# The first 12 alignments in four column blocks on 96 partitions, with rows joined through DRAM

## The chip, the cores and the metric

The kernel runs on one core of one Trainium2 chip. The metric is the device time of one execution in microseconds (us). Engines are named as in the profile: PE (TensorE), DVE (VectorE), ACT (ScalarE), POOL (GpSimd), SP (SyncE, which here only issues DMAs). Every engine works through its own instructions in a fixed order and waits at semaphores; 16 DMA engines move data.

## The reference, cut to what matters

The input x is 32 samples of 128 rows by 128 columns. Four steps update it: a gated attention, a quantized dense layer, an alignment (dynamic time warping) against ctx, and a mixture of 8 experts whose gates need one threshold over all 32 samples.

```python
x = x + tanh(g_xattn[0]) * _L0_xattn_ref(_layernorm(x), ctx_1024, ctx_1024, ...)
x = x + tanh(g_ffn[0])   * _L0_ffn_ref(_layernorm(x), W1, b1, W2, b2)
x = x + tanh(g_xattn[1]) * _L1_xattn_ref(ctx_1024, _layernorm(x))
x = x + tanh(g_ffn[1])   * _L1_ffn_ref(_layernorm(x), gate_weight, w1, b1, w2, b2)

def _align_one(small, large):                      # once for each of 32 samples
    D = sqrt(max(|small_i|^2 + |large_j|^2 - 2 small_i . large_j, 0))
    R[i, j] = D[i, j] + min(R[i-1, j], R[i, j-1], R[i-1, j-1])
    # walk back from the last corner to (0, 0): at each cell go to the smallest of
    # diagonal, up, left; every cell (i, j) on the way adds small[i] to expanded[j]
    return expanded
```

## The kernel before

**Before the alignment.** Attention and the first half of the quantized dense layer take the span up to about 220 us. The second half of the dense layer (`dense`, `second_dense`) is done in eight blocks of four samples, and each block's distances D follow from it. Samples 0 to 11 (blocks 0 to 2, `NP = 3`, `BP = 12`) are the first part, the other 20 the second part.

**Distances (L1134 to L1159).** For each of blocks 0 to 2, PE makes d2, DVE adds and clips (dd), ACT takes roots into `dist` (two buffers), and two DMAs write `dist` to `d_dram`, laid out as half, sample, row, column. Each sample is cut in two halves of `SH = 64` rows: the upper one from the top, the lower one upside down and reversed, so that both are scanned in the same direction. 12 samples by 2 halves are 24 lanes, one a partition.

**Rows (`warp_steps`, L955).** In chunks of 12 rows (the last has 4) SP loads the distances into `dc`. A row is two DVE instructions over 24 partitions by 128 columns: u = min(up, diagonal) at L1058, and a scan along the row, min with the left neighbour and add of the distance, at L1059. Results go into `ru`, as pairs (R, u) for each row.

**Tables (`tables`, L962).** The walk back needs for each cell the column in which the row above is reached. It is five DVE instructions over rows of R and u: dg (L975), to (L976), lf (L979), the scan vv (L982), dv (L986). To use more lanes, SP copies each finished chunk from `ru` to `rblk`, three rows to each of four partition groups (96 partitions, L1073), the tables are made while the next chunk is scanned, and SP moves dv back to 24 partitions into `DV` (memory of YT, L992).

**Meet and walk.** `meet` (L1000) turns the last rows by PE, joins the two halves and finds the cheapest crossing. `near`, the tables of the last four rows, is made on 24 partitions straight from `ru`. The walk is 63 dependent DVE instructions `hit` (L1087), one a row. Then PE turns the result (vt, ends_ps), and `ends` is ready (L1112). Ten matmuls `busy` (L953) run on PE shortly before the end of the walk; their result is not used.

**Beside it.** `second_dense` (from L1239) works through blocks 3 to 7 for the second part: ACT quantizes and takes norms and roots, PE makes po, tp and d, POOL adds, takes a power and stores the distances to `d_dram`. Its instructions are tied to one order on ACT (`last["act"]`) and PE (`last["pe"]`). Its place against the rows on PE and SP comes from the scheduler.

**After it.** The expert stage starts with `aligned(0)` (L1314) and the expert matmuls mph (L1494) and mpo (L1507). The second part's alignment (20 samples, 40 lanes) runs there in the background, with the same `warp_steps`; it begins with SP loading `dc` from `d_dram`.

What sets the order: within an engine, the scheduler puts instructions into one fixed order when the program is built, mostly in program order but by its own estimate of when an operand is ready; `tc.issue_after` adds an earliest place. DMAs take one of eight completion semaphores in turn, so that a ninth waits for the first.

Of the kernel before, what the change touches and what calls it, by code (L numbers as in the profile page):

```python
# [8 lines left out]
F32 = mybir.dt.float32  # L9
BF16 = mybir.dt.bfloat16  # L10
# [3 lines left out]
ALU = mybir.AluOpType  # L14
AX = mybir.AxisListType
# [3 lines left out]
P = 128  # L19
B = 32  # L20
S = 128
# [7 lines left out]
GB = 4  # L29
# [3 lines left out]
BIG = 1e30  # L33
SH = S // 2
# [3 lines left out]
NP = 3  # L38
BP = NP * GB
HELD = 34  # L40


@with_exitstack
def tile_flamingo_gated(
# [21 lines left out]
    nc = tc.nc  # L66
# [6 lines left out]
    def new(p, shape, dt, tag, bufs=None):  # L73
        kw = {} if bufs is None else {"bufs": bufs}
        return p.tile(shape, dt, tag=tag, name=tag, **kw)

    keep = pool(ctx, "keep")
    dram = pool(ctx, "dram", space=DRAM)
# [43 lines left out]
    ident = new(keep, [P, P], F32, "ident")  # L122
# [5 lines left out]
    rev = new(keep, [P, P], F32, "rev")  # L128
# [161 lines left out]
    with ExitStack() as st:  # L290
# [47 lines left out]
        for k in range(2):  # L338
# [5 lines left out]
                out=mtmp[:, k], in_=mtmp[:, k], compare_op=ALU.is_ge, fill=0.0,  # L344
# [444 lines left out]

    aa_s = new(rest, [P, B], F32, "aa_s")  # L790
    d_dram = new(dram, [2, B, SH, S], F32, "d_dram")
    parts = [ExitStack(), ExitStack()]
    HT = [None] * 4
    for k in (1, 0):
# [157 lines left out]
            with tc.issue_after(getattr(tie, "ins", tie)):  # L952
                tie = nc.tensor.matmul(busy, lhsT=onesb, rhs=w1q, start=True, stop=True)  # L953

    def warp_steps(s0, n_s, wp, w1p, ps_new, queue, DV, ends, lower, warmed=None):  # L955

        H2 = 2 * n_s
        BL = 2 if n_s > 16 else 4
        rows = max(n for _, n in CHUNKS)
        waiting = None  # L960

        def tables(rb, m, w, tag):  # L962


            lf, to = (new(w1p, [w, m, S + 1], BF16, t + tag) for t in ("lf", "to"))
            nc.vector.memset(lf[:, :, 0:1], 0.0)
            nc.vector.memset(to[:, :, 0:1], 0.0)
            dg = new(w1p, [w, m, S], BF16, "dg" + tag)
            vv = new(w1p, [w, m, S + 1], BF16, "vv" + tag)
            dv = new(w1p, [w, m, S], BF16, "dv" + tag)  # L970
            up = rb[:, 0:m, 0, 1 : S + 1]
            diag = rb[:, 0:m, 0, 0:S]
            left = rb[:, 1 : m + 1, 0, 0:S]
            least = rb[:, 1 : m + 1, 1, 0:S]
            nc.vector.tensor_tensor(dg, diag, up, ALU.is_le)  # L975
            nc.vector.tensor_tensor(  # L976
                to[:, :, 1:], jotab[0:w].unsqueeze(1).to_broadcast([w, m, S]), dg, ALU.subtract
            )
            nc.vector.tensor_tensor(lf[:, :, 1:], left, least, ALU.is_lt)  # L979


            nc.vector.tensor_tensor_scan(  # L982
                vv.rearrange("p r j -> p (r j)"), lf.rearrange("p r j -> p (r j)"),
                to.rearrange("p r j -> p (r j)"), 0.0, ALU.mult, ALU.min,
            )
            nc.vector.tensor_tensor(dv, vv[:, :, 1:], vv[:, :, 0:S], ALU.subtract)  # L986
            return dv

        def moved_tables(r0, m, rb):
            dv = tables(rb, m, BL * H2, "")  # L990
            for q in range(BL - 1, -1, -1):
                queue.dma_start(  # L992
                    out=DV[:, r0 + q * m : r0 + q * m + m, :], in_=dv[H2 * q : H2 * q + H2]
                )
# [1 line left out]
        vw = new(w1p, [H2, SH + 1], F32, "vw")  # L996
        nc.vector.memset(vw[:, 0:1], -2.0 * S)
        prev = None

        def meet(row):  # L1000

            gt_ps = ps_new([P, 2, n_s], "gt_ps")
            nc.tensor.transpose(gt_ps.rearrange("p h b -> p (h b)"), row, ident[0:H2, 0:H2])

            gt = new(w1p, [P, 2, 2, n_s], F32, "gt")
            nc.vector.tensor_copy(gt, gt_ps.unsqueeze(2).to_broadcast([P, 2, 2, n_s]))
            both_ps = ps_new([H2, 2, S], "both_ps")
            for h, where in ((0, ident), (1, rev)):
                nc.tensor.matmul(
                    both_ps[:, h, :], lhsT=gt[:, h].rearrange("p k b -> p (k b)"), rhs=where,  # L1010
                    start=True, stop=True,
                )
            far = new(w1p, [H2, S + 1], F32, "far")
            nc.vector.memset(far[:, S : S + 1], BIG)
            nc.vector.tensor_copy(far[:, 0:S], both_ps[:, 1, :])
            best = new(w1p, [H2, S], F32, "best")
            nc.vector.tensor_tensor(best, far[:, 0:S], far[:, 1 : S + 1], ALU.min)
            nc.vector.tensor_tensor(best, best, both_ps[:, 0, :], ALU.add)
            least = new(w1p, [H2, 1], F32, "least")
            nc.vector.tensor_reduce(least, best, AX.X, ALU.min)  # L1020
            to = new(w1p, [H2, S], F32, "far_to")
            nc.vector.tensor_tensor(to, far[:, 1 : S + 1], far[:, 0:S], ALU.is_le)
            nc.vector.scalar_tensor_tensor(to, to, 2.0, jota[0:H2], ALU.mult, ALU.add)
            cand = new(w1p, [H2, S], F32, "cand")
            nc.vector.scalar_tensor_tensor(cand, best, least, jota[0:H2], ALU.is_le, ALU.mult)
            mine = new(w1p, [H2, 1], F32, "mine")
            nc.vector.tensor_reduce(mine, cand, AX.X, ALU.min)
            got = new(w1p, [H2, 1], F32, "got")
            nc.vector.scalar_tensor_tensor(
                cand, jota[0:H2], mine, to, ALU.is_equal, ALU.mult, accum_out=got  # L1030
            )

            nc.vector.tensor_scalar(got, got, lower[:, 0:1], lower[:, 1:2], ALU.mult, ALU.add)
            nc.vector.scalar_tensor_tensor(
                vw[:, SH : SH + 1], mine, lower[:, 2:3], got, ALU.mult, ALU.add
            )

        for r0, n in CHUNKS:
            dc = new(wp, [H2, rows, S], F32, "dc")[:, 0:n, :]
            for v in (slice(0, 4), slice(4, n)) if r0 == 0 else (slice(0, n),):  # L1040
# [34 lines left out]
                    )  # L1075
                waiting = (r0, m, rb)
        yield 2.0
        meet(ru[:, n, 0, 1 : S + 1])
        yield 4.0
        near = tables(ru, n, H2, "_l")  # L1080
        yield 0.85 * n

        for r in range(SH - 1, 0, -1):
            hit = new(wp, [H2, S], BF16, "hit")
            nc.vector.scalar_tensor_tensor(  # L1087
                hit, jotab[0:H2], vw[:, r + 1 : r + 2],
                near[:, r - r0, :] if r >= r0 else DV[:, r, :], ALU.is_le, ALU.mult,
                accum_out=vw[:, r : r + 1],  # L1090
            )
            if warmed is not None and r == 12:
                idle(warmed, None, hit, 10)
            yield 0.39

        vt = ps_new([SH, 2, 2, n_s], "vt")
        for k in range(2):
            nc.tensor.transpose(
                vt[:, k].rearrange("p h b -> p (h b)"), vw[:, k : SH + k], ident[0:H2, 0:H2]
            )  # L1100
        ev = new(w1p, [SH, 2, 2, n_s], F32, "ev")
        nc.vector.tensor_copy(ev[:, 0], vt[:, :, 0])
        for k in range(2):
            nc.vector.tensor_scalar(
                ev[:, 1, k, :], vt[:, 1 - k, 1], -1.0, -2.0 * S - 2.0, ALU.mult, ALU.add
            )
        ends_ps = ps_new([P, 2, n_s], "ends_ps")
        for h, where in ((0, ident), (1, rev)):
            nc.tensor.matmul(
                ends_ps, lhsT=where[0:SH, :], rhs=ev[:, h], start=(h == 0), stop=(h == 1)  # L1110
            )
        nc.vector.tensor_copy(ends, ends_ps)  # L1112
        yield 1.0

    ends = [new(rest, [P, 2, n], F32, f"ends{n}_{k}") for k, n in enumerate((BP, B - BP))]

# [1 line left out]
    with ExitStack() as st:  # L1118
# [18 lines left out]
        for g, ym2, ysq in normed:  # L1137
            d2 = new(dps, [P, GB, S], F32, "d2")
            nc.tensor.matmul(d2, lhsT=ones, rhs=ysq, start=True, stop=False)  # L1139
            for i in range(GB):  # L1140
                nc.tensor.matmul(
                    d2[:, i, :], lhsT=CD[:, GB * g + i, :], rhs=ym2[:, i, :],
                    start=False, stop=(i == GB - 1),
                )
            dd = new(dp, [P, GB, S], F32, "dd")
            for i in range(GB):
                b = GB * g + i
                nc.vector.tensor_scalar(
                    dd[:, i, :], d2[:, i, :], aa[:, b : b + 1], 0.0, ALU.add, ALU.max
                )  # L1150
            dist = new(dp, [P, GB, S], F32, "dist")
            nc.scalar.activation(dist[0:SH], dd[0:SH], AF.Sqrt)
            got = nc.scalar.activation(dist[SH:P], dd[SH:P, :, ::-1], AF.Sqrt)
            held["root"] = getattr(got, "ins", got)
            for h in range(2):
                (nc.sync, nc.scalar if g == NP - 1 else nc.sync)[h].dma_start(
                    out=d_dram[h, GB * g : GB * g + GB].rearrange("b r j -> r b j"),
                    in_=dist[SH * h : SH * h + SH],
                )  # L1159
    parts[0].close()  # L1160


# [1 line left out]
    with ExitStack() as st:  # L1164
# [123 lines left out]
                d2 = distance_product(n, ym2, ysq)  # L1288
            roots(NG - 1, d2)

        for _ in warp_steps(
            0, BP, wp, w1p, lambda shape, tag: new(w_ps, shape, F32, tag), nc.sync,
            DV, ends[0], masks[0], new(w_ps, [P, HID], F32, "busy"),
        ):
            pass
# [270 lines left out]
```

## Time and profile before

| what | us |
|---|---|
| three runs | 858.38, 862.26, 864.83 |
| median | 862.26 |
| profiled execution: span | 854.5 |
| profiled execution: own time | not given; median less span is 7.8 |
| DVE busy / PE busy / ACT busy in the span | 591.8 / 690.8 / 449.7 |

The places of the stage in the profiled span:

| event | us |
|---|---|
| first store of distances issued on SP | 248.02 |
| first row scan | 258.77 |
| last row done, turned by PE (gt_ps) | 322.04 |
| first hit / first hit that reads moved tables | 328.47 / 334.13 |
| last hit done | 357.8 |
| ends written | 359.9 |
| first expert matmul (mph) | 370.24 |

How to read it: the profile gives busy time, idle time before an instruction and the releaser that ended it. A busy share over the whole span says little about this stage: from 248 to 358 us PE is mostly idle and DVE is nearly full; after 370 us PE is full and DVE has room.

### The profile page before, as it was taken

How to read it: one execution, taken by the hardware profiler on the slowest of the kernel's cores; microseconds unless marked ns; L12 is line 12 of the kernel's file. 1: busy time of each engine (PE TensorE's matmuls, PEld its weight loads, DVE VectorE, ACT ScalarE, POOL GpSimd, SP SyncE). 2: the span in 40 equal slices, each digit the busy share in tenths (PEclk: the TensorE clock that was granted, in tenths of full speed). 3: DMA queues.
4: the chain of work that ended last, by engine and by line, in shares of the span. 5: the costliest groups of instructions: out<-in, count | busy, mean ns of one | idle time of the engine just before them, and what ended most of it. 6: DMA issues, size and time to landing. Idle time of an engine off the chain costs nothing.

```text
span 854.5 us, 13313 instructions
## 1 busy us (share of the span) xinstructions
PE 690.8 (81%) x4721; PEld 459.1 (54%) x4721; DVE 591.8 (69%) x2052; ACT 449.7 (53%) x791; POOL 66.7 (8%) x132
## 2 busy tenths in 40 slices
PE   5798998344242435589999999999999999999997
PEld 2244454211231223257777777766777777777776
DVE  7757999879858998889993666656705544444444
ACT  3787877496258888334444443443443433434332
POOL 2000000000401221100101010010010000000000
PEclk9897999555565555699999999999999999999999
DMA  8100000200021221023543020020013112121110
GB/s 326 38 2 13 2 3 2 80 20 0 0 42 36 55 61 32 13 60 98 157 138 100 38 87 25 38 74 32 31 63 87 50 37 87 38 65 56 52 51 26
DMA packets 20201, 47.32 MB, mean 55 GB/s; under 512 B 4014, under 2 KB 6942, under 8 KB 20110
## 3 DMA queue, kind: packets, MB, share of 16 engines
q1 hardware_dynamic: 14372, 29.69, 11.4%
q0 software_dynamic: 5056, 16.62, 6.2%
q8 instruction: 37, 0.61, 0.3%
q10 hardware_dynamic: 706, 0.16, 0.1%
q14 instruction: 30, 0.25, 0.1%
HBM read 27.12 MB, written 13.37 MB: 47 GB/s over the span
## 4 chain that ended last, share of the span: by engine, by line
PE 55%; DVE 20%; issue 2%; DMA 1%; ACT 1%; POOL 0%; SPq 0%; DVEq 0%; ACTq 0%
PE mph L1494 25%; PE mpo L1507 25%; DVE ru L1059 4%; DVE ru L1058 3%; DVE hit L1087 2%; DVE hst L858 2%; DVE hst L859 2%; PE px L1328 1%; PE small L1357 1%; PE px L1351 1%; DVE junk L1371 1%; PE po L916 1%; DMA d_dram<-dist 1%; PE busy L953 0%; PE d L1139 0%
## 5 line engine op out<-in xcount | busy, mean ns | idle before, releaser
L1507 PEld LDWEIGHTS mpo<-mw,hT 128*128 128x128 f32 x2048 | 249.7, 192 | 58.9 <-issue 39.7
L1499 ACT ACTIVATE hT<-mph,mb1s 128x512 f32<-128x512 f32 x256 | 175.6, 687 | 181.9 <-PE mph L1494 168.4
L1507 PE MATMUL mpo<-mw,hT 128*128 128x128 f32 x2048 | 256.3, 276 | 0.1
L1494 PE MATMUL mph<-YT,mw 128*128 128x512 f32 x512 | 244.1, 597 | 0.0
L1494 PEld LDWEIGHTS mph<-YT,mw 128*128 128x128 f32 x512 | 87.2, 192 | 57.9 <-issue 57.8
L1457 DVE TENSOR_TENSOR biased<-mpo,mb2s 128x512 f32<-128x512 f32 x28 | 19.4, 691 | 119.6 <-PE mpo L1507 119.6
L1462 DVE SCALAR_TENSOR_TENSOR X<-biased,GA,X 128x128 f32<-128x128 f32 x248 | 67.8, 344 | 0.1
L1515 ACT COPY ye<-mpo 128x512 f32<-128x512 f32 x34 | 19.9, 585 | 86.1 <-PE mpo L1507 83.5
L1059 DVE TENSOR_TENSOR_SCAN ru<-ru,dc 24x128 f32<-24x128 f32 (+1 forms) x128 | 54.0, 422 | 6.9 <-DMA dc<-d_dram 3.2
L1058 DVE TENSOR_TENSOR ru<-ru 24x128 f32<-24x128 f32 (+1 forms) x128 | 38.9, 304 | 3.2
L1516 POOL DMA_DIRECT2D y_dram<-ye x34 | 18.5, 543 | 224.9 <-ACT ye L1515 224.5
L562 ACT ACTIVATE dm<-bi 128x512 f32<-128x512 f32 x48 | 28.8, 603 | 7.9 <-PE bi L557 2.7
L604 DVE TENSOR_TENSOR sm<-sc,dm 128x512 f32<-128x512 f32 x32 | 21.7, 682 | 12.8 <-ACT dm L562 9.7
L1209 PE MATMUL po<-w2q,HT 128*128 128x128 bf16 x80 | 9.4, 311 | 25.5 <-ACT HT L1182 25.5
L849 PE MATMUL ph<-XQ,w1q 128*128 128x512 bf16 x32 | 15.8, 616 | 16.6 <-DVE XQ L840 9.2
L1276 PE MATMUL tp<-ident,y 128*128 128x128 f32 x20 | 8.1, 474 | 22.6 <-ACT y L1182 22.6
L1087 DVE SCALAR_TENSOR_TENSOR hit<-jotab,vw,YT 24x128 bf16<-24x128 bf16 x59 | 21.1, 357 | 4.1 <-DMA YT<-dv 2.0
L518 ACT ACTIVATE qm<-YT,mcol 128x512 f32<-128x512 f32 x32 | 23.1, 729 | 0.0
L1457 DVE TENSOR_TENSOR biased<-yl,mb2s 128x512 f32<-128x512 f32 x34 | 23.1, 680 | 0.0
L1209 PEld LDWEIGHTS <-HT 128*128 128x128 bf16 x80 | 8.1, 144 | 26.9 <-ACT HT L1182 26.9
L215 PE MATMUL at<-ident,y 128*128 128x128 f32 x32 | 8.1, 374 | 17.3 <-DVE y L211 16.9
L1087 DVE SCALAR_TENSOR_TENSOR hit<-jotab,vw,CD 40x128 bf16<-40x128 bf16 x59 | 20.3, 344 | 2.1
(389 smaller groups left out, 1021.0 us busy)
## 6 DMA issues: line engine op xcount, KB each, us to landing
y_dram<-ye POOLq DMA_DIRECT2D x34, 256.0 KB, 2.3
yl<-y_dram SPq DMA_DIRECT2D x34, 256.0 KB
mw<-in_mw POOLq DMA_DIRECT2D x12, 512.0 KB, 4.5
rblk<-ru SPq DMA_DIRECT2D x10, 288.8 KB
X<-in_x SPq DMA_DIRECT2D x4, 512.0 KB
CD<-in_ctx_d SPq DMA_DIRECT2D x4, 512.0 KB
CT<-in_ctx_t SPq DMA_DIRECT2D x4, 512.0 KB
mw<-in_mw SPq DMA_DIRECT2D x4, 512.0 KB
```

The costliest lines, as they stand in the source:

```text
L518: nc.scalar.activation(held["qm", g][:, h], YT[:, GB * g : GB * g + GB, :], AF.Copy, scale=mcol[:, h : h + 1],)
L562: done = nc.scalar.activation(dm, bi, AF.Exp)
L604: got = nc.vector.tensor_tensor(sm, scs[:, u], dm, ALU.mult)
L1058: nc.vector.tensor_tensor(u, ru[:, r, 0, 1 : S + 1], ru[:, r, 0, 0:S], ALU.min)
L1059: got = nc.vector.tensor_tensor_scan(ru[:, r + 1, 0, 1 : S + 1], u, dc[:, r, :], BIG, ALU.min, ALU.add)
L1087: nc.vector.scalar_tensor_tensor(hit, jotab[0:H2], vw[:, r + 1 : r + 2], near[:, r - r0, :] if r >= r0 else DV[:, r, :], ALU.is_le, ALU.mu ...
L1457: nc.vector.tensor_tensor(t, y, bias, ALU.add)
L1462: nc.vector.scalar_tensor_tensor(X[:, b, :], v[:, i, :], GA[:, E * b + e : E * b + e + 1], X[:, b, :], ALU.mult, ALU.add,)
L1494: got = nc.tensor.matmul(ph, lhsT=w1e[:, j, c * P : (c + 1) * P], rhs=tok, start=True, stop=True)
L1499: got = nc.scalar.activation(hT[c], ph, AF.Gelu_apprx_tanh, bias=mb1s[:, e, c : c + 1])
L1507: got = nc.tensor.matmul(po[:, i, :], lhsT=hT[c][:, i * S : (i + 1) * S], rhs=w2e[:, j, c, :], start=(c == 0), stop=(c == NC - 1),)
L1515: nc.scalar.copy(ye, po)
```

## The change

The first part's alignment gets a function of its own, `sections`; the second part keeps `warp_steps`, whose pieces `tables`, `meet` and `walk_steps` become functions that both use.

The 128 columns of each lane are cut into four blocks of 32 (`NQ = 4`, `W4 = 32`). A lane and a block have a partition of their own: 96 partitions. Each block is four rows behind its left neighbour (`LAG = 4`), so one instruction handles four different rows, and 64 rows take `STEPS = 64 + 3 * 4 = 76` steps. Every four steps a shuffle across partitions and a maximum hand the last column of a block to its right neighbour. The distances go to DRAM as `d_part`, with 32 columns in a run; the last block's store is cut into rows 0 to 15 and 16 to 63. A finished row lies on four partitions, so the rows are written to DRAM (`r_part`) and read back for the tables: three times 20 rows, four to each of five partition groups (120 partitions), and four near rows on 24 partitions.

```diff
+NQ = 4
+W4 = S // NQ
+LAG = 4
+STEPS = SH + (NQ - 1) * LAG
...
+    d_part = new(dram, [2 * BP, NQ, SH, W4], F32, "d_part")
+    r_part = new(dram, [2 * BP, SH, 2, S], F32, "r_part")
+    lanes = 2 * BP * NQ
+    leftmost = new(rest, [lanes, 2], F32, "leftmost")
+    nc.vector.tensor_reduce(leftmost[:, 1:2], ident[0:lanes, 0:lanes:NQ], AX.X, ALU.max)
...
+    def sections(wp, w1p, ps_new, queue, DV, ends, lower, warmed):
+
+        H2, L = 2 * BP, 2 * BP * NQ
+        BL, m = 5, 4
+        near_0 = SH - m
+        dc = new(w1p, [L, STEPS, W4], F32, "dcs")
+        nc.gpsimd.memset(dc[:, 0 : (NQ - 1) * LAG, :], 0.0)
+        nc.gpsimd.memset(dc[:, SH:STEPS, :], 0.0)
+        ru = new(w1p, [L, STEPS + 1, 2, W4 + 4], F32, "rus")
...
+        for v in (slice(0, 4), slice(4, 16), slice(16, SH)):
+            for q in range(NQ):
+                queue.dma_start(
+                    out=dc[q:L:NQ, LAG * q + v.start : LAG * q + v.stop, :], in_=d_part[:, q, v, :]
+                )
...
+        def fetch(b, to, r):
+            a = 1 if r == 0 else 0
+            queue.dma_start(
+                out=to[H2 * b : H2 * b + H2, a : m + 1, 1 : 2 * S + 1].rearrange(
+                    "z r (k s) -> z r k s", k=2
+                ),
+                in_=r_part[:, r + a - 1 : r + m],
+            )
+
+        def moved_tables(r0):
+            dv = row_tables(rb, BL * H2, "")
+            for b in range(BL - 1, -1, -1):
+                queue.dma_start(
+                    out=DV[:, r0 + b * m : r0 + b * m + m, :], in_=dv[H2 * b : H2 * b + H2]
+                )
+
+        stops = (20, 40, 52, 60, SH)
+        for t in range(STEPS):
+            u = ru[:, t + 1, 1, 1 : W4 + 1]
+            nc.vector.tensor_tensor(u, ru[:, t, 0, 1 : W4 + 1], ru[:, t, 0, 0:W4], ALU.min)
+            got = nc.vector.tensor_tensor_scan(
+                ru[:, t + 1, 0, 1 : W4 + 1], u, dc[:, t, :], ru[:, t + 1, 0, 0:1], ALU.min, ALU.add
+            )
+            if t % LAG == LAG - 1 and t + 1 < STEPS:
+                edge = new(wp, [L, LAG], F32, "edge")
+                nc.vector.stream_shuffle(
+                    edge, ru[:, t + 2 - LAG : t + 2, 0, W4], [i - 1 if i % NQ else i for i in range(32)]
+                )
+                got = nc.vector.tensor_scalar(
+                    ru[:, t + 2 : t + 2 + LAG, 0, 0], edge, leftmost[:, 0:1], None, ALU.max
+                )
+            yield 0.45
+            for q in range(NQ):
+                end = t + 1 - LAG * q
+                if end in stops:
+                    r = (0, *stops)[stops.index(end)]
+                    queue.dma_start(
+                        out=r_part[:, r:end, :, W4 * q : W4 * q + W4],
+                        in_=ru[q:L:NQ, r + LAG * q + 1 : end + LAG * q + 1, :, 1 : W4 + 1],
+                    )
+                    if q == NQ - 1:
+                        if end in (20, 40, 60):
+                            for b in range(BL):
+                                fetch(b, rb, end - 20 + m * b)
+                        elif end == SH:
+                            fetch(0, rn, near_0)
+            if t in (49, 69):
+                with tc.issue_after(getattr(got, "ins", got)):
+                    moved_tables(20 * (t // 60))
+
+        def turned(to):
+            for q in range(NQ):
+                nc.tensor.matmul(
+                    to[W4 * q : W4 * q + W4], lhsT=ru[:, SH + LAG * q, 0, 1 : W4 + 1],
+                    rhs=ident[0:L, q:L:NQ], start=True, stop=True,
+                )
+
+        met = meet(turned, BP, w1p, ps_new, lower, vw)
+        with tc.issue_after(met):
+            moved_tables(40)
+            near = row_tables(rn, H2, "_l")
+        for w in walk_steps(
+            BP, wp, w1p, ps_new, vw,
+            lambda r: near[:, r - near_0, :] if r >= near_0 else DV[:, r, :], ends, warmed,
+        ):
+            yield w
...
-            for h in range(2):
-                (nc.sync, nc.scalar if g == NP - 1 else nc.sync)[h].dma_start(
-                    out=d_dram[h, GB * g : GB * g + GB].rearrange("b r j -> r b j"),
-                    in_=dist[SH * h : SH * h + SH],
-                )
+            for v in (slice(0, 16), slice(16, SH)) if g == NP - 1 else (slice(0, SH),):
+                for h in range(2):
+                    (nc.sync, nc.scalar if g == NP - 1 else nc.sync)[h].dma_start(
+                        out=d_part[BP * h + GB * g : BP * h + GB * g + GB, :, v, :].rearrange(
+                            "b q r w -> r (b q) w"
+                        ),
+                        in_=dist[SH * h + v.start : SH * h + v.stop].rearrange(
+                            "r b (q w) -> r (b q) w", w=W4
+                        ),
+                    )
...
-        for _ in warp_steps(
-            0, BP, wp, w1p, lambda shape, tag: new(w_ps, shape, F32, tag), nc.sync,
+        for _ in sections(
+            wp, w1p, lambda shape, tag: new(w_ps, shape, F32, tag), nc.sync,
             DV, ends[0], masks[0], new(w_ps, [P, HID], F32, "busy"),
```

## The prediction

> **What bounds the kernel now.** I read the chain that ended last first. Over the span it is PE matmuls of the expert stage, but between 238 and 375 us another engine carries it:
>
> ```profile
> by line: DVE ru L1059 19.1%; DVE ru L1058 15.4%; DVE hit L1087 13.6%; issue 7.8%; DMA d_dram<-dist 3.6%; PE busy L953 2.9%; PE mph L1494 2.7%; PE d L1139 2.6%; DMA dc<-d_dram 2.1%; DVE lf L979 1.8%; DVE dg L975 1.5%; PE px L1328 1.5%; PE tp
> ```
>
> So the alignment of the first 12 samples is the bound there: the row scans (ru), then the walk (hit). The first expert matmul starts at 370.24, right behind it; a shift of this stage's end shifts the whole. Next the timeline of each engine, for prices and for who stands beside it (start, us, engine, line, what, idle before it and who ended that):
>
> ```profile
> 258.77 0.41 DVE L1059 TENSOR_TENSOR_SCAN ru<-ru,dc 24x128 f32<-24x128 f32 x1 [3.24 <-DMA dc<-d_dram]
> 259.22 0.28 DVE L1058 TENSOR_TENSOR ru<-ru 24x128 f32<-24x128 f32 x1
> 241.41 0.16 DVE L188 TENSOR_TENSOR root_t<-bn_r 128x4 f32<-128x4 f32 x1
> 320.98 0.67 DVE L975 TENSOR_TENSOR dg_l<-ru 24x512 bf16<-24x512 f32 x1
> 322.98 1.22 DVE L982 TENSOR_TENSOR_SCAN vv_l<-lf_l,to_l 24x516 bf16<-24x516 bf16 x1
> 334.13 0.34 DVE L1087 SCALAR_TENSOR_TENSOR hit<-jotab,vw,YT 24x128 bf16<-24x128 bf16 x1 [2.04 <-DMA YT<-dv]
> 359.74 0.18 DVE L1112 COPY ends<-ends_ps 128x24 f32<-128x24 f32 x1 [1.28 <-PE ends_ps L1109]
> 297.76 0.69 ACT L1182 ACTIVATE t<-po,s 128x512 f32<-128x512 f32 x1
> 351.77 0.60 ACT L1182 ACTIVATE b<-tp 128x512 f32<-128x512 f32 x1 [2.39 <-DMA d_dram<-b]
> 291.57 1.89 PE L1209 MATMUL po<-w2q,HT 128*128 128x128 bf16 x16 [3.45 <-ACT HT L1182]
> 332.11 3.00 SPq L992 DMA_DIRECT2D YT<-dv  x4
> 365.60 2.23 SPq L1042 DMA_DIRECT2D dc<-d_dram  x6
> ```
>
> What to see: a row costs a TT of 0.28 and a scan of 0.41, with pitches 0.32 and 0.45. The last L982 row starts its scan of 516 elements at 322.98, inside the meet. ACT's second dense stage runs beside all of it and ends (ysq of block 7) at 352.4, 5 us ahead of the last hit at 357.8: it is hidden, but barely. SP moves tables (YT) early, and only at 365.6, after everything, fetches the second part's distances.
>
> Last, the DMA windows of the distance store (share and GB/s are the last two columns):
>
> ```profile
> 250.00:251.00 1.00, 0.00 (x0) 0.00 (x0) 0.50 (x2) 0.01 (x1) 0.00 (x0) 1.00 1.03 205
> ```
>
> All 16 engines are full with 512 B packets: 16 x 512 / 205 = 40 ns each; the trace's packet records give 45 (median). The same records have 27 ns for a 512 B load and 13 ns for a 128 B load.
>
> **The change part by part.**
>
> *Rows.* 64 steps of 0.77 become 76 of 32 elements. The scan's slope is (1.22-0.41)/(516-128) = 2.1 ns an element, so 0.41-0.20 = 0.21; TT's is (0.67-0.28)/384 = 1.0 ns, so 0.18. With the gaps 0.25+0.22 = 0.47. Over 76: 35.4. The 18 edges are a shuffle and a TENSOR_SCALAR of 4 elements. No shuffle is in the trace; the 4-element row takes 0.16 at a pitch of 0.20, and one of the two overlaps the next TT: 0.30 an edge, 5.4 (bounds 0.06, the smallest memset, and 0.54, a table row of 384: -4 to +4 us in all). With two of the 1 us hiccups that the row timeline has every 16 to 20 us (263.80, 279.39): 43. Before, rows with four tables among them took 258.77 to 322.0 = 63. That is the gain: 20 us, half of it only because the tables are out.
>
> *Distances.* Six stores of 256 packets of 512 B become 6144 packets of 128 B: 384 an engine, not 96. A 128 B write to DRAM is not in the trace. Bounds: 13 ns (the load) and 90 (twice the 512 B write). I take the load's 13 plus what a 512 B write costs over a load, 45-27 = 18: **31 ns**. Then 249.4 + 11.9 + 0.5 = 261.8 for landing (data started at 249.4; the last packet to release took 0.5 at 251.39). The built order makes the first load of dcs wait for all eight pieces, the 48-row ones too. From landing to first scan before: 254.48 to 258.77, 4.3. First scan at 266.1, 7.3 late. Rows end at 266.1+42.8 = 308.9.
>
> The Trainium skill (DMA: Bandwidth & Descriptors, Specifications) says that below 512 B the DMA engine does a read-modify-write, which speaks against this change; the measured rows cannot show it. Worked out as a load plus a write of these rows, 13+45 = 58 ns, the sum below would end 11 us later, near 916.
>
> *Tables, and what the built order does to them.* In the order in which the changed program issues instructions, DVE has all 76 rows, then meet, then all three blocks of tables one after the other, then the near rows, then the hits. The 20 us of rows come without any table below them, so nothing hides tables any more: each block is (by 512-element rows) 0.67+0.67+0.41+1.22+0.45, with overlap 3.3, after a meet of 6.5 (321.99 to 328.47). And SP has them in program order: five YT<-dv of block 0 stand before the row stores of rows 20 to 40 of the last column block, which stand before the fetch of block 1, and so on. So SP stands still from its second store of rows 20 to 40 until block 0 is done, then must store, land, fetch, land, for block 1, again for block 2. At 0.72 an issue (the 0.75 of YT<-dv), 24-row copies on 12 engines (the packet records show 12 completions for a rblk copy):
> meet 315.4, block 0 318.7; 5 issues 322.3; 128 packets an engine at 31 ns plus 1.8: 328.1; five fetches and a DRAM load, 3.6+2.2: 333.9; block 1 337.2; 14 more stores and moves, 272 packets, 8.4, then 5.8 for the fetch, about 351; block 2 about 354.
>
> *The last wait.* On SP the fetch of the near rows stands behind three dc<-d_dram loads of the second part, and these wait for the last d_dram<-b, which is the end of ACT's second dense stage. Before, that load stood at the end of SP's queue and delayed nobody; now the walk waits for it. And this stage is itself made later: on PE the first gt_ps matmul (it waits for step 63) stands before po of block 5, which ran at 291.57. Step 63 ends 12 x 0.54 before the rows: 302.4; po 1.9: 304.3; t at 304.4, not 297.76: 6.6 late. From there to the end nothing changes: ysq of block 7 ends at 352.4+6.6 = 359.0; d(7) at PE's half clock 3.8 (2.08+1.91 overlapped, as at 337.56): 362.8; from its roots to SP's release 360.88 to 365.60, 4.7: 367.5; three loads 1.1, near fetch 2.9 (dc: issue 255.82 to 258.68): 371.5; near tables 3.1: 374.6; 63 hits at 0.385 and one hiccup 25.3: 399.9; 2.1 to ends (357.8 to 359.9): **402.0, against 359.9: 42.1 us late.**
>
> *The rest.* Eight small memsets on POOL lie in its 37.95 us of idle time before 263.75; without that cover they are 1 to 2 us. Three leftmost instructions on DVE (under 0.5) come in the attention stage. `busy` comes in the same place before the experts. The expert stage is untouched.
>
> The page gives the profiled execution's span (854.5) and not its own time; the median of the three runs is 862.26 (858.38 to 864.83), 7.8 around the span. I add the shift to the median: **904**.
>
> By the price of a 128 B write: 13 ns gives rows 259.7 to 302.5, no delay by PE worth the name, a shift of 35.7 (898). 45 ns: first scan 271.5, PE 12 late, 47.5 (910). 90 ns: first scan 288.8, meet 338.3, and now the tables' chain through SP is last: 341.6, 345.2, 358.5, 364.3, block 1 367.6, stores to about 388, fetch 394, block 2 397, near 400, hits 425, ends 428: 68 (930).
>
> **The rivals.**
>
> *Not slower: SP is never in the way.* If the copies arrive before meet ends, only DVE counts: rows end 308.9, meet 315.4, three blocks and near 13, hits 25.3, 2.1: 355.8, 4 us early, 858; with the 13 ns price 852, and with tables between the rows some 10 less, 846. It decides if the near fetch lands before 325. For it: the scans do get shorter, 63 to 43. Against: the near fetch stands behind dc<-d_dram, and the row of before at 365.60 shows when that is let go.
>
> *Slow stores bind.* From about 70 ns a packet the SP chain is later than the second dense stage: 916 to 935. For it: writes of 512 B already cost 1.7 times a load. Against: the 13 ns of small loads.
>
> *A smaller loss.* The dense stage ends sooner because PE is not held and d(7) no longer stands behind `busy`: 4 to 12 us less, 885 to 898.
>
> **How the numbers follow.** Forecast (898 to 916, walk waits for the near fetch) 0.68; slow stores 0.20; smaller loss 0.07; not slower 0.05, of which 0.03 gains over 1%. About 1% (8.6 us) is what a measurement here can tell from none. The range leaves out half of the slow stores' far end and the rival: 893 to 933. Faster 0.03, same 0.02, slower 0.95.
>
> **What would show it.** In the new profile: rows at 0.47 a step; three L975 groups of 120x512 after meet, each with an idle time ended by DMA rblk<-r_part; near's dg_l idle until DMA rnear<-r_part, right after dc<-d_dram on SP; PE idle until gt_ps in the 290s; first scan near 266. Wrong: tables between rows, or near's wait under 5 us.

## The result, and the profile after

The changed kernel takes 897.29 us (median of 4 runs, 895.57 to 899.24), the kernel before on the same chip 860.82 (4 runs, 858.38 to 864.83). The ratio is 1.0431, with a 95% interval of 1.0394 to 1.0468: slower by 36.5 us. The profiled execution has a span of 893.9, against 854.5.

The chain that ended last, between 238 and 415 us of the changed kernel, by line:

```profile
by line: DVE hit L1032 12.1%; DVE rus L1187 11.6%; issue 10.6%; ACT HT L1306 9.0%; ACT y L1306 8.1%; DVE rus L1186 6.3%; DMA d_dram<-b 4.7%; DMA d_part<-dist 2.9%; PE mph L1618 2.2%; PE d L1258 2.0%; POOL d_dram L1360 1.9%; PE px L1452 1.8%
```

The rows take 17.9% of a window of 177 us (rus), where they took 34.5% of one of 137 us (ru): 32 us in place of 47. New in the chain are ACT HT and ACT y, which are the second dense stage, and its stores d_dram<-b. A stage that was hidden beside the rows now stands in the chain.

SP's own queue through the stage (start, us, line, what, how many issues):

```profile
249.52 5.00 SPq L1276 DMA_DIRECT2D d_part<-dist  x6
257.53 9.12 SPq L1157 DMA_DIRECT2D dcs<-d_part  x12
...
289.56 2.05 SPq L1203 DMA_DIRECT2D r_part<-rus  x2
318.28 3.83 SPq L1179 DMA_DIRECT2D YT<-dv  x5
322.15 2.39 SPq L1203 DMA_DIRECT2D r_part<-rus  x3
326.21 1.99 SPq L1169 DMA_DIRECT2D rblk<-r_part  x5
...
343.19 0.76 SPq L1203 DMA_DIRECT2D r_part<-rus  x1
366.05 1.47 SPq L1086 DMA_DIRECT2D dc<-d_dram  x3
367.62 0.30 SPq L1169 DMA_DIRECT2D rnear<-r_part  x1
368.02 3.87 SPq L1179 DMA_DIRECT2D YT<-dv  x5
```

Two holes are to be seen. From 291.6 to 318.28 SP waits with the first move of block 0's tables, while finished rows 20 to 40 wait behind it. From 343.95 to 366.05 it waits with dc<-d_dram, with the fetch of the near rows right behind. SP's waits name what it waits for there (what was waited for, us in total, times, longest); the first line is the kernel before, where the same load waits longer, but stands last in the queue and holds nobody:

```profile
SPq L1042 <- DMA d_dram<-b: 30.3, 1, 30.3
```

```profile
SPq L1086 <- DMA d_dram<-b: 22.3, 2, 21.9
```

d_dram<-b is the store of the second part's distances, the end of each block of the second dense stage. DVE's timeline shows the other side of both holes (the bracket is the idle time before, and who ended it):

```profile
260.68 0.28 DVE L1187 TENSOR_TENSOR_SCAN rus<-rus,dcs 96x32 f32<-96x32 f32 x1 [1.43 <-DMA dcs<-d_part]
260.99 0.19 DVE L1186 TENSOR_TENSOR rus<-rus 96x32 f32<-96x32 f32 x1
261.21 0.28 DVE L1187 TENSOR_TENSOR_SCAN rus<-rus,dcs 96x32 f32<-96x32 f32 x1
...
314.89 0.69 DVE L975 TENSOR_TENSOR dg<-rblk 120x512 bf16<-120x512 f32 x1
331.97 0.69 DVE L975 TENSOR_TENSOR dg<-rblk 120x512 bf16<-120x512 f32 x1 [13.68 <-DMA rblk<-r_part]
346.76 0.69 DVE L975 TENSOR_TENSOR dg<-rblk 120x512 bf16<-120x512 f32 x1 [11.39 <-DMA rblk<-r_part]
370.21 0.68 DVE L975 TENSOR_TENSOR dg_l<-rnear 24x512 bf16<-24x512 f32 x1 [20.08 <-DMA rnear<-r_part]
373.57 0.34 DVE L1032 SCALAR_TENSOR_TENSOR hit<-jotab,vw,dv_l 24x128 bf16<-24x128 bf16 x1
...
399.03 0.18 DVE L1056 COPY ends<-ends_ps 128x24 f32<-128x24 f32 x1 [0.56 <-PE ends_ps L1053]
```

A scan and its TT have a pitch of 0.54 us. The rows end at 308.5; all three blocks of tables and the near rows come after the meet, and DVE stands idle for 13.7, 11.4 and 20.1 us between them. The walk itself is 63 hits in 24.2 us, at the 0.34 us a hit of before.

The profiles do not start this stage at the same moment: the first distance store lies between 247.9 and 256.6 us. So experiments are compared from the first distance store on: to SP's fetch of the near rows, to the first hit, and to the first px matmul of the expert stage, which reads the walk's end. The times come from different rounds, in which the kernel before took 856.1 to 860.8 us; the ratio is against the kernel before of the same rounds.

| kernel | time, us | ratio to before (95%) | near fetch | first hit | first px |
|---|---|---|---|---|---|
| before | 860.82 | | none | 80.5 | 112.9 |
| changed | 897.29 | 1.0431 (1.0394 to 1.0468) | 118.1 | 124.1 | 150.7 |
| near_first | 877.3 | 1.0216 (1.0147 to 1.0285) | 97.1 | 103.7 | 130.3 |
| wide_store | 894.65 | 1.0389 (1.0296 to 1.0483) | 113.8 | 119.9 | 146.6 |
| wide_hold | 893.8 | 1.0418 (1.0384 to 1.0452) | 117.7 | 123.8 | 150.5 |
| pe_free | 892.54 | 1.0396 (1.0328 to 1.0464) | 116.1 | 122.2 | 149.1 |
| three_orders | 862.43 | 1.0054 (1.0032 to 1.0075) | 77.5 | 84.0 | 117.3 |
| moves_last | 861.72 | 1.0055 (1.0035 to 1.0076) | 71.2 | 78.3 | 116.9 |
| moves_last_pe_bound | 868.47 | 1.0131 (1.0099 to 1.0163) | 71.4 | 97.8 | 125.4 |
| busy_first | 853.56 | 0.9943 (0.9917 to 0.9970) | 70.7 | 78.3 | 108.1 |

The changed kernel's stage is 150.7 - 112.9 = 37.8 us longer, and it starts 1.5 us later (249.52 against 248.02): together 39.3, the difference of the spans (39.4).

### The profile page after: what moved, and what is told of

It is laid out like the page before. It is cut to its first block, busy times and chain, and to the rows that moved or that the text cites. A ratio compares the mean times of both kernels' runs of the same rounds, so it can differ in the third digit from the quotient of the medians.

```text
span 893.9 us, 13386 instructions
## 1 busy us (share of the span) xinstructions
PE 694.1 (78%) x4728; PEld 461.4 (52%) x4728; DVE 582.5 (65%) x2099; ACT 450.0 (50%) x791; POOL 68.0 (8%) x140
## 4 chain that ended last, share of the span: by engine, by line
PE 59%; DVE 25%; ACT 9%; issue 4%; DMA 2%; POOL 1%; DVEq 0%; SPq 0%; ACTq 0%; POOLq 0%
PE mph L1618 24%; PE mpo L1631 24%; DVE hit L1032 2%; DVE rus L1187 2%; DVE hst L870 2%; DVE hst L871 2%; ACT HT L1306 2%; PE at L458 2%; ACT y L1306 2%; DVE rus L1186 1%; DVE sm L609 1%; PE px L1452 1%; DVE bn L160 1%; DMA d_dram<-b 1%; PE sc L543 1%
## 5 line engine op out<-in xcount | busy, mean ns | idle before, releaser
L1618 PEld LDWEIGHTS mph<-YT,mw 128*128 128x128 f32 x512 | 86.9, 192 | 57.9 <-issue 57.8
L1477 ACT COPY YT<-px 128x512 f32<-128x512 f32 x8 | 4.7, 586 | 51.0 <-PE px L1475 51.0
L1103 DVE TENSOR_TENSOR_SCAN ru<-ru,dc 40x128 f32<-40x128 f32 x64 | 26.6, 416 | 1.5
L1187 DVE TENSOR_TENSOR_SCAN rus<-rus,dcs 96x32 f32<-96x32 f32 x76 | 23.2, 305 | 4.1 <-DMA dcs<-d_part 1.4
L975 DVE TENSOR_TENSOR dg<-rblk 80x768 bf16<-80x768 f32 (+1 forms) x8 | 6.8, 847 | 25.1 <-DMA rblk<-r_part 25.1
L1342 PE MATMUL d<-b,ones 128*128 128x512 f32 x10 | 10.3, 1134 | 15.0 <-ACT b L1306 15.0
## 6 DMA issues: line engine op xcount, KB each, us to landing
y_dram<-ye POOLq DMA_DIRECT2D x34, 256.0 KB, 2.3
yl<-y_dram SPq DMA_DIRECT2D x34, 256.0 KB
```

The costliest lines, as they stand in the source:

```text
L1103: got = nc.vector.tensor_tensor_scan(ru[:, r + 1, 0, 1 : S + 1], u, dc[:, r, :], BIG, ALU.min, ALU.add)
L1187: got = nc.vector.tensor_tensor_scan(ru[:, t + 1, 0, 1 : W4 + 1], u, dc[:, t, :], ru[:, t + 1, 0, 0:1], ALU.min, ALU.add)
L1618: got = nc.tensor.matmul(ph, lhsT=w1e[:, j, c * P : (c + 1) * P], rhs=tok, start=True, stop=True)
```

## The experiments

The theory: the loss is one of order, and the last link is SP's queue, where the fetch of the near rows stands behind dc<-d_dram and so behind the end of ACT's second dense stage. Rivals: the row stores and fetches on SP are slow; the 128-byte writes are slow; the scans on 96 partitions are.

**near_first: the near rows' fetch ahead of dc<-d_dram.** `held["near"]` is the fetch of rnear, `held["moved"]` the last move of block 2's tables.

```diff
                 for h in range(2):
-                    queue.dma_start(
+                    with tc.issue_after(held["near"]), tc.issue_after(held["moved"]):
+                        queue.dma_start(
...
```

> Only an order on SP's queue differs from the changed kernel: the second part's loads dc<-d_dram are queued behind the fetch of the near rows and the last table moves, not ahead of them. Theory (the walk waits for the near rows, and these stand behind dc<-d_dram, which waits for the end of ACT's second dense stage): the near rows land near 350, just as block 2's tables end (350.1 in the trace of the changed kernel), near tables 3.1, hits from 353.3 and not 373.6, ends_ps 20 us earlier; time about 877. Rival A (the chain of table moves, row stores and fetches on SP is what the walk waits for): near lands no more than 5 us earlier, time 892 to 897. Rival B (the row scans and the 128-byte packets are the loss): no change.

SP's queue and DVE's timeline of near_first:

```profile
345.43 0.76 SPq L1205 DMA_DIRECT2D r_part<-rus  x1
349.09 0.29 SPq L1170 DMA_DIRECT2D rnear<-r_part  x1
352.37 3.85 SPq L1180 DMA_DIRECT2D YT<-dv  x5
368.28 2.57 SPq L1087 DMA_DIRECT2D dc<-d_dram  x6
```

```profile
334.21 0.69 DVE L975 TENSOR_TENSOR dg<-rblk 120x512 bf16<-120x512 f32 x1 [13.50 <-DMA rblk<-r_part]
348.98 0.69 DVE L975 TENSOR_TENSOR dg<-rblk 120x512 bf16<-120x512 f32 x1 [11.36 <-DMA rblk<-r_part]
352.26 0.67 DVE L975 TENSOR_TENSOR dg_l<-rnear 24x512 bf16<-24x512 f32 x1
```

dg_l has no idle time before it any more, dc<-d_dram still leaves at the end of the dense stage and holds nobody, and the first hit comes 124.1 - 103.7 = 20.4 us sooner; 877.3 was expected as about 877. Against the kernel before of the same rounds the loss falls from 4.3% to 2.2%. Rivals A and B fall for this part. The two waits for rblk stand as they were: they are the next link.

**wide_store and wide_hold: distances stored with 512 bytes a packet.**

```diff
-    d_part = new(dram, [2 * BP, NQ, SH, W4], F32, "d_part")
+    d_part = new(dram, [2 * BP, SH, S], F32, "d_part")
...
-                    out=dc[q:L:NQ, LAG * q + v.start : LAG * q + v.stop, :], in_=d_part[:, q, v, :]
+                    out=dc[q:L:NQ, LAG * q + v.start : LAG * q + v.stop, :], in_=d_part[:, v, W4 * q : W4 * q + W4]
```

> d_part keeps whole rows of 128 elements, so that its stores write 512 bytes a packet again, as before the change, and the loads into the 96 partitions take 128 bytes a packet. Theory (a 128-byte write costs little more than the 13 ns of a 128-byte load, and the end of the second dense stage, not the rows, sets the walk): the first scan comes 0 to 1.5 us earlier than 260.7, the near rows' wait ends where it did, time 896 to 898. Rival (small writes are slow and cost the rows their start): first scan 4 us or more earlier, and the time follows by as much.

The first scan came 10.7 us after the first store, against 11.2: 0.5 sooner, as the theory says. The time, 894.65, comes from four runs between 888.15 and 898.5 and tells little. But the near fetch came 4.3 us sooner, which nobody expected. The scheduler had moved something else too: with other DMAs ahead, it put gt_ps behind po of block 5 on PE. wide_hold keeps the wide stores and ties PE to the changed kernel's order (`gt0` and `gt3` are the first and last gt_ps, `both` is both_ps, n is the block):

```diff
+            if n == 5:
+                last["pe"] = held["gt0"]
...
-            with tc.issue_after(last["pe"]):
+            with tc.issue_after(last["pe"] if n != 4 else held["gt3"]):
                 nc.tensor.matmul(d2, lhsT=ones, rhs=ysq, start=True, stop=False)
+            with tc.issue_after(last["pe"] if n != 4 else held["both"]):
...
```

> wide_store also came with another order on PE: its gt_ps matmuls stand behind po of block 5. Here the 512-byte stores are kept and PE's order is that of the changed kernel, gt_ps ahead of po of block 5, so that this kernel differs from the changed one in the stores alone, and from wide_store in PE's order alone. Times counted from the first distance store, where the near rows' fetch is issued at 118.1 in the changed kernel and at 113.8 in wide_store. Theory (the stores' size is worth nothing, the 4.3 us of wide_store are PE's hold on the second dense stage): t of block 5 waits 3 to 4 us for po again, the fetch is issued at 117 to 118.5; time 896 to 899. Rival (the 512-byte stores brought the 4.3 us): the fetch stays at 114 to 115, time 892 to 894.

ACT's timeline, t of block 5, first in wide_store, then in wide_hold:

```profile
306.10 0.69 ACT L1304 ACTIVATE t<-po,s 128x512 f32<-128x512 f32 x1
```

```profile
301.04 0.69 ACT L1306 ACTIVATE t<-po,s 128x512 f32<-128x512 f32 x1 [3.38 <-PE po L1335]
```

With PE's order back, the wait of 3.4 us is back and the fetch is at 117.7: 3.9 of the 4.3 us are PE's hold on the dense stage, 0.4 may be the stores. The time, 893.8, lies below the 896 to 899 expected and in the 892 to 894 of the rival. It decides nothing: the ratio's interval overlaps the changed kernel's, and the stage up to the first px takes 150.5 us, against 150.7. Only the trace separates these kernels.

**pe_free: gt_ps behind po of block 5 on PE.** Program order is changed so that the dense stage up to po of block 5 comes ahead of the meet; `last["pe"]` is that po at the first tie:

```diff
+                with tc.issue_after(last["pe"]):
                     nc.tensor.matmul(
                         to[W4 * q : W4 * q + W4], lhsT=ru[:, SH + LAG * q, 0, 1 : W4 + 1],
...
         met = meet(turned, BP, w1p, ps_new, lower, vw)
+        last["pe"] = held["both"]
```

> Only an order on PE differs from the changed kernel: the matmuls gt_ps, which wait for step 63, stand behind po of block 5, not ahead of it; the transposes of block 5 stand behind the meet. Theory (gt_ps holds po, so t of block 5 and everything of the second dense stage behind it, and the near rows wait for that stage's end): t of block 5 starts 3 to 5 us earlier than 302.62, the near rows' wait ends 3 to 5 us earlier, time 892 to 894. Rival (the dense stage has slack, or the wait for the near rows is not set by it): t earlier, time unchanged.

t of block 5 came 3.3 us sooner (49.8 after the first store, against 53.1), the near fetch only 2.0 (116.1 against 118.1). So the hold counts, but my tie had put the transposes of block 5 behind the meet and gave part of it back; wide_store, where the scheduler put these transposes ahead of the last gt_ps, kept the whole 4.3 (they start 57.9 after the first store there, 64.3 in pe_free). The median of 892.54 is in the expected range, but the ratio's interval takes in the changed kernel's 1.0431, so the time alone proves nothing.

**all_three: all orders at once, with a mistake.** Here the fetch of a block stands ahead of the tables of the block before it, so that block 0's and block 1's tables are built from the next block's rows: this is not the alignment, and only its times are read.

> The order of near_first, the order of pe_free, and two blocks of tables put between the rows: rows from step 54 on stand behind block 0's tables, those from step 72 on behind block 1's. Theory (all of the loss is order: the rows themselves are shorter than before): rows end near 315 with two blocks of tables among them, meet near 321, block 2 near 324.5, near rows land near 325, near tables end near 328.5, walk ends near 355, against 399.8; time about 852, below the kernel before. Rival (the scans on 96 partitions or the joining through DRAM cost more than they save): walk ends after 362, time 862 or more.

It took 877.01 us and missed: the first px came at 121.7. DVE waited 8.2 us for the second fetch before block 0's tables, and PE's tie made the dense stage wait for a meet that had become late: t of block 6 came 92.0 us after the first store, against 72.6 in the changed kernel. Tying one engine's order to another's moves the wait if the other one is late.

**three_orders: the same with the fetch behind the tables.** Two things differ from all_three: the tables stand behind steps 49 and 69 in program order, as in the changed kernel, and not behind 53 and 71, where the next block's fetch already stood ahead of them; and gt_ps stands behind the transposes of block 5, not behind po of block 5. The rows are tied to the tables in both:

```diff
+            with tc.issue_after(held["tabled"]) if t in (54, 72) else ExitStack():
+                nc.vector.tensor_tensor(u, ru[:, t, 0, 1 : W4 + 1], ru[:, t, 0, 0:W4], ALU.min)
```

> What all_three was to be, with each block's tables built before the next block is fetched: the order of near_first; two blocks of tables among the rows (rows from step 54 on behind block 0's tables, those from step 72 on behind block 1's); gt_ps and both_ps on PE behind the transposes of block 5 and ahead of po of block 6. On SP the five table moves of block 0 still stand ahead of the last row stores of rows 20 to 40. Theory (all of the loss is order): block 1's tables wait about 2 us for their fetch, block 2's tables end near 329, near rows land near 332, walk from 335, ends near 359.5 on the changed kernel's clock, where it ends at 399.8; time 857 (853 to 862), about that of before. Rival (scans on 96 partitions and joining through DRAM cost more than they save): walk ends after 366, time 864 or more.

The first hit is at 84.0, where 85.5 was worked out (335), but from there to the first px it takes 33.2 us, and in the changed kernel 26.7. So 862.43 just misses the range, and the end of the walk, 365.7 on the changed kernel's clock, lies at the rival's 366: this run alone doesn't tell the theory from the rival. One thing was missing in the sum; the next experiment shows it larger.

**moves_last: the moves of a block's tables behind the next block's stores and fetch.**

```diff
-                    moved_tables(20 * (t // 60))
+                    dv = row_tables(rb, BL * H2, "")
+            if t == 51:
+                moves(0, dv, held["fetched"])
+            elif t == STEPS - 1:
+                moves(20, dv, held["near"])
```

> three_orders, and on SP the table moves of a block stand behind the row stores and the fetch of the next block (those of block 1 behind the fetch of the near rows). Theory (what is left in three_orders is SP's own order): no wait of DVE for rblk or rnear above 2 us, near rows land near 321, meet ends near 321, block 2 324.5, near tables 327.7, walk ends near 354 on the changed kernel's clock; time 852, 5 us below three_orders and below the kernel before. Rival: the moves are hidden, time as three_orders.

All waits for rblk and rnear are gone, and the first hit is at 78.3, another 5.7 us sooner and 2.2 us sooner than in the kernel before. Yet the time is that of three_orders, 861.72. The 5.7 us went into a wait in the middle of the walk. DVE's timeline has it, and PE's shows what it waits for:

```profile
363.90 0.34 DVE L1034 SCALAR_TENSOR_TENSOR hit<-jotab,vw,YT 24x128 bf16<-24x128 bf16 x1 [10.40 <-PE busy L960]
```

```profile
359.86 2.07 PE L1356 MATMUL d<-b,ones 128*128 128x512 f32 x2 [5.63 <-ACT b L1320]
361.73 1.91 PE L1358 MATMUL d<-a,CD 128*128 128x128 f32 x8
363.58 0.28 PE L960 MATMUL busy<-hit,onesb 24*128 24x128 bf16 x1
```

`busy`, whose result nobody uses, reads the hit of row 12. There are two hit buffers, so the hit two rows on has to wait until busy has read. On PE busy stands behind d of block 7, and this waits for ACT. In three_orders the same wait is 5.70 us (at 358.90), in moves_last 10.40: the walk, come early, waits again for the end of the second dense stage, by another way.

**moves_last_pe_bound: moves_last without the tie on PE.** The meet's matmuls go where the scheduler puts them. I had read one block too few: the last gt_ps and both_ps stand behind po of block 7, not 6.

> moves_last without the order on PE: there the last gt_ps and both_ps stand behind po of block 6. Theory (an order on PE can hold the meet as it held the dense stage): both_ps not before po of block 6 is done, near 324.5, meet ends near 328.5, walk ends near 361.5; time 859, 7 us above moves_last. Rival (po of block 6 is early enough): same as moves_last within 1%.

PE's timeline:

```profile
336.00 1.89 PE L1343 MATMUL po<-w2q,HT 128*128 128x128 bf16 x16 [3.45 <-ACT HT L1316]
337.81 0.30 PE L1229 MATMUL gt_ps<-ident,rus 96*32 96x24 f32 x2
338.42 0.62 PE L998 MATMUL both_ps<-ident,gt 128*24 128x128 f32 x2 [0.30 <-DVE gt L995]
```

The mechanism holds, and its size follows the block: the rows end at 318.2, but both_ps starts at 338.42, which is 86.3 from the first store and not 75 as expected (66.8 in moves_last). The first hit comes 19.5 us later than in moves_last, the first px only 8.5, because moves_last's 10.4 us of waiting in the walk fall away: here busy stands where nothing holds it. So it is in part luck that the time lies 6.8 us above moves_last, where 7 were expected: both_ps came 11 us later than worked out, and the 10.4 us of waiting, not in the sum, fell away. The rival's mark, within 1%, is met too (0.8%), but its reason is not: po does hold the meet.

**busy_first: d of block 7 behind the end of the walk on PE.** `held["walked"]` is the last ends_ps.

```diff
-            with tc.issue_after(last["pe"]):
+            with tc.issue_after(held["walked"] if n == NG - 1 else last["pe"]):
```

> moves_last, and on PE d of block 7 stands behind the end of the walk (busy, vt, ends_ps), as it does in the kernel before; in moves_last busy stands behind d, and a hit waits 10.4 us for busy to have read the hit of row 12. Theory (that wait is the last one left, and behind it the second dense stage): the walk has no idle time above 1 us, ends_ps about 357 to 358 with the first store of the distances at 253.3 (367.8 in moves_last), then d of block 7 from 360 to 364 and the first px at 364 instead of 370: 6 us, time 855 to 857, the kernel before within 0.5%. Rival (the walk's end is not what the expert stage waits for): same as moves_last, 861 to 862.

PE's timeline:

```profile
351.92 0.28 PE L960 MATMUL busy<-hit,onesb 24*128 24x128 bf16 x1
352.13 4.45 PE L965 MATMUL busy<-w1q,onesb 128*128 128x512 bf16 x10
356.51 0.30 PE L1044 MATMUL vt<-ident,vw 24*64 24x24 f32 x2
...
357.63 1.13 PE L1357 MATMUL d<-b,ones 128*128 128x512 f32 x2
358.59 1.05 PE L1359 MATMUL d<-a,CD 128*128 128x128 f32 x8
359.48 1.06 PE L1478 MATMUL px<-CT,pt 128*128 128x128 f32 x8
```

The hit's wait falls from 10.4 to 0.6 us, and the first px from 116.9 to 108.1. The median is 853.56, against 858.68 of the kernel before in the same rounds: ratio 0.9943 (0.9917 to 0.9970), the only version whose interval lies below the kernel before; it is a gain of 0.6%. The first px comes 2.6 us sooner than worked out (364 is 110.7 from the first store), since d of block 7 costs 1.13 and 1.05 here, not 2.07 and 1.91.

## Why the prediction was right

It named the mechanism (the walk waits for the near rows, these for dc<-d_dram, this for ACT's second dense stage), and near_first shows it alone: one order on one queue, 20 us of the 36.5. Most signs it gave are there: three L975 groups of 120x512 behind the meet, dg_l held until rnear right behind dc<-d_dram, and PE idle until gt_ps at 300.45, which is 299.0 on the forecast's clock (the sign said the 290s, its own sum 302.4). Of the three groups only the second and third waited for rblk<-r_part; the first came straight behind the meet, as the sum had it and the sign did not. Two signs were not there: rows at 0.47 a step and a first scan near 266. Its time, 904 with a range of 893 to 933, lay 6.7 us above the measured median, which falls just below the 898 to 916 of the main forecast. Point by point, with the trace's times less the 1.5 us by which the stage starts later:

| step of the prediction | forecast | trace, less 1.5 |
|---|---|---|
| distances landed | 261.8 | 256.0 |
| first scan | 266.1 | 259.2 |
| rows, first scan to end | 43 | 47.8 |
| block 0's tables done | 318.7 | 316.8 |
| block 1, block 2 done | 337.2, 354 | 333.8, 348.6 |
| t of block 5 later than before | 6.6 | 3.4 |
| SP released for dc<-d_dram | 367.5 | 364.6 |
| near tables done | 374.6 | 372.0 |
| ends | 402.0 | 397.7 |

- *Distances.* The term "31 ns a packet" was too large: 128-byte writes took 11 ns in the median on SP's queue (5120 packet records) and 13 on ACT's (1024), less than my lower bound of 13. The window row of the changed kernel (the last two columns are the DMA share and GB/s) shows full engines:

```profile
251.00:252.00 1.00, 0.00 (x0) 0.00 (x0) 1.00 (x4) 0.56 (x1) 0.00 (x0) 1.00 1.08 187
```

  16 x 128 / 187 = 11 ns, and nearly the 205 GB/s of the 512-byte stores of before. wide_hold bears it out: with 512 bytes a packet the first scan comes 0.5 us sooner, and no more. The Trainium skill (DMA: Bandwidth & Descriptors, Specifications) says that below 512 bytes the DMA engine does a read-modify-write. No view here shows whether it reads; the price seen is small: four 128-byte writes took 44 ns, one of 512 bytes 45 in the kernel before and 32 in wide_store. By this term alone the sum should have been the 898 of its 13 ns line.
- *Rows.* "0.47 a step" was too small: 0.54. The TT took 0.19 (0.18 was worked out), the scan 0.28 and not 0.21. Of a scan I had two rows, of 128 elements in f32 and of 516 in bf16, and drew one slope through them; from 128 to 32 elements of f32 it is (0.41-0.28)/96 = 1.35 ns an element, not 2.1. The Trainium skill (VectorE: DVE Perf Modes, The TRN2 errata) gives a measured fixed part of about 150 cycles of 0.96 GHz beside one cycle an element; for the TT that makes, as an estimate, 190 ns at 32 elements, and the trace has 190. An edge cost 0.24, not 0.30 (four steps with one take 2.40). 76 x 0.54 + 18 x 0.24 = 45.4, and the rest of the 47.8 are hiccups such as the scan of 1.21 at 265.47. (76 steps of 0.47 are 35.7, not the 35.4 of the sum.)
- *PE's hold.* Foreseen, at 6.6 us; 3.4 at t of block 5, and 3.9 at the near fetch (wide_store against wide_hold). The 13 ns line had "no delay by PE worth the name"; with the longer rows step 63 came at 300.4, and there was one.
- *What cancelled.* The first scan was 6.9 us sooner, the rows 4.8 longer; so the tables, the near rows and the walk all came within 2 to 5.5 us of the forecast. The size of the loss was right in part because two terms were wrong in opposite directions.
- *From spans to medians.* I added the shift to a median that lies 7.8 above the profiled span. Wherever the record has both, an execution's own time is 1.7 or 1.8 above its span (895.57 and 893.9 in the changed kernel), so the profiled execution of before took some 856.2 and was quicker than its median; the spans differ by 39.4, the medians by 36.5.

Of the rivals, "slow stores bind" fell (11 ns, wide_hold). "A smaller loss", 885 to 898, takes in the measured 897.29, but not by its reason: PE did hold the dense stage, only for less than worked out, and d of block 7 stood free of `busy` in the main sum already. "Not slower: SP never in the way" was worked out at 846 to 858; with the orders mended, busy_first takes 853.56. So the change has a gain of some 5 us in it (5.1 in busy_first), and the order in which it was built turns it into a loss of 36.5. The traces give two causes why the gain is no larger. The first hit comes only 2.2 us sooner (78.3 against 80.5). In moves_last the rows with two blocks of tables among them take 55.0 (264.4 to 319.4), against 63.2 before, and the meet 4.7, against 6.5; but the third block and the near tables, 7.4 us (324.18 to 331.6), now stand between meet and walk. And the second dense stage is close behind as the next bound: in busy_first its last ysq ends at 357.46, and the walk's `ends` is written at 357.9. That a shorter walk alone would gain nothing more is read from these rows and was not tried.

What stays open: where the 1 us hiccups of the rows come from, why 512-byte writes took 45 ns in the kernel before and 32 in wide_store, and whether other widths than 32 columns or another lag would pay; no run here tells.

## What to carry to other kernels

A DMA queue is a line: before moving a transfer that a short path needs, list what stands ahead of it in the built order and when that is released; here one load with nothing to do with the walk cost 20 us. When a change shortens a stage, ask what was hidden behind it with how much slack, for that limits what there is to gain; here the second dense stage ended 5.4 us ahead of the last hit in the kernel before (352.4 and 357.8), and the best version gained 5.1 (that the one sets the other was not tried). And a mended wait has to be followed to the next one: three_orders and moves_last differ by 5.7 us at the first hit and by nothing in time, because an unused matmul held a buffer.

## What was not expected of the hardware

- 128-byte writes to DRAM took 11 ns each, a quarter of what 512-byte writes took in the kernel before (45 in the median; 32 in wide_store): the bytes a second were nearly the same (187 and 205 GB/s). In wide_store 202 GB/s kept the engines busy for 0.80 of the time only.
- How long SP needs for an issue does not follow the bytes: 0.77 us for a move of YT (24 KB; five in 3.83), 0.76 in the mean for the loads of dcs (twelve in 9.12), but 0.40 for a rblk and 0.30 for rnear (120 KB each).
- The same two d matmul groups took 2.07 and 1.91 us in moves_last and 1.13 and 1.05 in busy_first, where they run shortly behind ten filler matmuls. The granted clock differs by about as much: 0.50 from 359.8 to 363.6 us in moves_last and 1.00 from 357.6 to 359.5 in busy_first. Whether the fillers raised it was not tried alone.
